# A Mamba and mixture-of-experts layer on one core: gelu's bias, the last sequence's logits and the start of the sixth expert group

## The chip, the core and the metric

The kernel runs on one core of a Trainium2 chip. The metric is the device time of one execution in microseconds; of several runs the median is given. The profile comes from one further execution, recorded by the hardware.

## What is computed

Sixteen sequences of 512 tokens with 256 features pass through two layers. All is in fp32.

```python
# layer 1: bidirectional state-space block (inner width 512, 16 states)
xf, res = split(x @ in_proj_w.T)
xf = silu(causal_conv(xf));  y = ssm(xf) * silu(res)
xb = silu(causal_conv_b(xf)); y = y + ssm_reversed(xb) * silu(res)
x = layernorm(x + y @ out_proj_w.T)
# layer 2: soft mixture of 16 experts, 64 slots each (1024 slots)
xn = layernorm(x) * norm_g + norm_b
se = (layernorm(slot_embeds) * slot_g + slot_b) * scale
logits   = einsum("bnd,esd->bnes", xn, se)
dispatch = softmax(logits, over tokens)
combine  = softmax(logits, over all slots)
slots = einsum("bnd,bnes->besd", xn, dispatch)
gate = gelu(slots @ Wg + bg);  up = slots @ Wu + bu
eout = (gate * up) @ Wd + bd
x = layernorm(x + combine @ eout)
```

The same logits feed two softmaxes: dispatch normalizes over the tokens, combine over the slots.

## The kernel before

**The scan.** `seq_layers` walks through the sequences 0 to 15. Each has four parts, `scan_part`: two directions for each half of the 512 channels. A part has eight pairs of states times two channel blocks, so a sequence has 64 scan steps. In a step ScalarE (ACT) makes decays and tanh factors (L453, L455), GpSimd (POOL) two products of 128x1024 elements (L436, L465), VectorE (DVE) the scans (L459, L461) and a product (L464), and TensorE (PE) turns the results and adds them up in PSUM (L380). A matmul with a tile of zeros (L376) opens each accumulator.

**Work beside the scan.** Everything else is written as generators, which `Side` objects hold in three queues: `prep` (the next scan part's inputs), `front` (`finish`: output projection, normalization, then `dispatch`) and `back` (`experts` and `combine`). After each scan step `beside_scan` lets them take a piece. `front` and `back` are paced: a queue's credit grows at each step by its remaining pieces over the remaining steps, which `begin(n)` sets. Instructions marked `late` stay in the order in which the program issues them; the scheduler places the others.

**Groups.** The experts of two sequences are done together: group g holds the sequences 2g and 2g+1. When the loop is at sequence b, `back` is given group (b-2)//2 at b = 3, 5, ..., 13 and, as a special case, the sixth group at b = 14: `experts(g, 0, 8)` (eight pairs of experts), then the combination of both sequences. `back.begin` gets 128 steps at odd b, 100 at b = 14, 64 at b = 15. In the last sequence (`hurry`) gaps between pieces aren't kept.

**One pair of experts.** Weights are loaded by SyncE's queue (SP), 512 KB each, into three buffers in the scan. `pg`: a matmul of the bias rows with a pattern of ones from the identity (L847), then the slots times Wg (L852). ACT makes the gelu of 128x512 (L869, L872). `pu`: the slots times Wu (L796). DVE adds bu and multiplies (L808). `peo`: times Wd (L823). DVE adds bd (L888) and the result goes to DRAM (L889). The slots `st` come from DRAM into a single buffer (L779).

**Logits.** `dispatch` computes them with the slots on the partitions, eight blocks `pl` of 128 slots x 512 tokens (L699), takes the maximum (DVE, L704), exp (ACT, L710), reciprocal and scale, turns the result (L716) and multiplies by the tokens (`pq`, L731); the slots go to DRAM as `sl`. `weights`, for the combination, computes the logits once more with the tokens on the partitions: for 128 tokens two halves `cl` of 512 slots (L906) from x2, which `finish` stored to DRAM and `load_x2` brings back. Then maxima (L914, L915), exp (L920), a turn `ctp` (L927), a copy `ct` (L936), and `combine` multiplies by the experts' outputs, `cpo` (L988), adds x1 (L997) and normalizes.

**The tail.** After the scan its PSUM and SBUF are given back: eight PSUM banks and eight weight buffers (`wide`) are then there. `front` still has `finish` and `dispatch` of sequence 15, `all_weights` of 14 and 15 (all turned weights kept) and the combination of 15; `back` has what is left of group 6, `experts` of group 7 and the combination of 14. Both are taken up in turn without pacing.

Of the kernel before, what the change touches and what calls it, by code (L numbers as in the profile page):

```python
# [9 lines left out]
F32 = mybir.dt.float32  # L10
# [7 lines left out]
P = 128  # L18
L = 512
# [36 lines left out]
def seq_layers(tc, ident, neghalf, a, out):  # L56
# [22 lines left out]
    with ExitStack() as ctx:  # L79
# [49 lines left out]
            return tc.keep_in_program_order(ins)  # L129


        zeros = const.tile([P, L], BF16, name="zeros")
        nc.vector.memset(zeros, 0.0)

        unit = const.tile([XW, 1], F32, name="unit")
# [234 lines left out]
        def add_up(depth):  # L370
            while len(pending) > depth:
                first, unit, last, c, hc, accs, w, u, name, done = pending.pop(0)
                if first:
                    accs[c] = ps_acc.tile([P, L], F32, tag="acc", name=name)

                    late(nc.tensor.matmul(accs[c], zeros[:, :P], zeros, start=True, stop=False))  # L376
                for j in range(2):
                    for lc in range(NL):
                        s = slice(lc * P, (lc + 1) * P)
                        ins = nc.tensor.matmul(  # L380
                            accs[c][:, s],
                            hc[:, j, s],
                            ident,
                            is_transpose=True,
                            start=False,
                            stop=(last and j == 1 and lc == NL - 1),
                        )
# [174 lines left out]
        def moe_setup():  # L562

            sg, sb = channels(a["slot_g"], "slot_g"), channels(a["slot_b"], "slot_b")
            scale = const.tile([P, 1], F32, name="scale")
            nc.sync.dma_start(scale, a["scale"].unsqueeze(0).to_broadcast([P, 1]))
            for t in (sg, sb):
                late(nc.vector.tensor_scalar(t, t, scale, None, ALU.mult))
            ses, src = [], a["slot_embeds"].rearrange("e s d -> (e s) d").rearrange("(h c p) d -> h p c d", p=P, c=4)
            for h in range(NSC // 4):  # L570
                se = p2.tile([P, 4 * DM], F32, tag="W", name=f"se_{h}", bufs=3)
                se = se.rearrange("p (c d) -> p c d", c=4)
                nc.sync.dma_start(se, src[h])
                ses.append(se)
            yield 0
            stats = [factors(row_moments(nc, p2, se, "m1", late), "m1") for se in ses]
            yield 0
            for se, (rs, sh) in zip(ses, stats):
                scaled(se, se, sh, rs)
            for k in range(NM):  # L580
                for h in range(NSC // 4):
                    yield 1
                    pt = bank(f"pse_{k}_{h}")
                    for j in range(4):
                        nc.tensor.transpose(pt[:, j * P : (j + 1) * P], ses[h][:, j, k * P : (k + 1) * P], ident)
# [6 lines left out]
            for key in ("bu",):  # L592
                rows = p2.tile([NE * NF, P], F32, tag="fr", name=f"{key}_rows")
                nc.sync.dma_start(rows, a[key].rearrange("e (c p) -> (e c) p", p=P))
# [6 lines left out]
                biases[key] = t  # L601

        def factors(mv, tag):

# [17 lines left out]
        def finish(b, y):  # L622
# [50 lines left out]
            for k in range(NM):  # L673
# [13 lines left out]
            yield from dispatch(b, xn, x2T)  # L687

        dispatched = {}
        expert_done = set()  # L690

        def dispatch(b, xn, x2T):

            for sc in range(NSC):
# [58 lines left out]
        def experts(g, lo, hi):  # L753
# [52 lines left out]
            def times(e, ht, pu):  # L806
                for fc in range(NF):
                    ins = nc.vector.scalar_tensor_tensor(  # L808
                        ht[:, fc, :],
                        pu[:, fc * P : (fc + 1) * P],  # L810
                        biases["bu"][:, e * NF + fc : e * NF + fc + 1],
                        ht[:, fc, :],
                        ALU.add,
                        ALU.mult,
                    )
                    if fc == 0:
                        late(ins)
# [15 lines left out]
            for ep in range(lo, hi):  # L833
# [5 lines left out]
                    yield WAIT  # L839
                yield 2  # L840
                pgs = []
                for j in range(2):
                    e = e0 + j
                    pg = bank(f"pg_{g}_{e}")

                    own = ident[: NE * NF, e * NF : (e + 1) * NF].unsqueeze(2).to_broadcast([NE * NF, NF, P])
                    nc.tensor.matmul(  # L847
                        pg.rearrange("p (f s) -> p f s", f=NF), biases["bg"], own, start=True, stop=False
                    )
                    for fc in range(NF):  # L850
                        for k in range(NM):
                            nc.tensor.matmul(  # L852
                                pg[:, fc * P : (fc + 1) * P],
                                got["Wg", e][:, k, fc * P : (fc + 1) * P],
                                st[:, k, :, j * SL : (j + 1) * SL],
                                start=False,
                                stop=(fc == NF - 1 and k == NM - 1),
                            )
                    pgs.append(pg)
                used[0] += 2  # L860
# [36 lines left out]
        def weights(b, lc, x2, keep):  # L897

            i = f"{b}_{lc}"
            yield 2  # L900
            t = x2.pop()
            cls = []
            for h in range(2):
                cl = bank(f"cl_{i}_{h}")
                for k in range(NM):
                    nc.tensor.matmul(  # L906
                        cl, t[:, k, :], seT[:, k, h * 512 : (h + 1) * 512], start=(k == 0), stop=(k == NM - 1)
                    )
                cls.append(cl)
            if lc + 1 < NL:  # L910
# [31 lines left out]
            return cts, sm[:, 2:3]  # L942

        def all_weights(b, kept):
            x2 = [load_x2(b, 0)]
            yield 0
            for lc in range(NL):
                kept[b, lc] = yield from weights(b, lc, x2, True)
# [72 lines left out]
        for b in range(nb):  # L1021
            bwd, nxt, accs = {}, {}, {}


            if 3 <= b < nb - 1 and b % 2 == 1 or b == nb - 2:
                g = (b - 2) // 2
                back.add(8 * PAIR, experts(g, 0, 8))
                back.add(COMBINE, combine(2 * g))
                back.add(COMBINE, combine(2 * g + 1))
            hurry = b + 1 == nb  # L1030
            front.begin(64)
            back.begin(128 if b % 2 == 1 and b + 1 < nb else 100 if b == nb - 2 else 64)

            def gate(c, b=b, accs=accs, bwd=bwd):
                y = bwd["res"]
# [85 lines left out]
```

## Time and profile before

| what | us |
|---|---|
| median of 3 runs | 5352.24 (5351.16 to 5356.49) |
| profiled execution | 5353.58 |
| its span, first to last instruction | 5351.8 |
| POOL busy | 4680.8 |
| DVE busy | 4551.7 |
| PE busy | 4331.0 |
| ACT busy | 4089.7 |
| last scan result added up (L1036) | 5100.7 |

The span is the time from the first to the last instruction; the execution's own time is 1.8 us longer. Busy time says how long an engine had instructions running; a matmul's end is modelled and neighbouring matmuls overlap, so starts are the safer measure on PE. `128x512` in a row is partitions by elements; `xN` counts instructions. One fp32 matmul of the program stands as two in the profile, a transpose as one. `<-` in a row of waits names what ended the wait.

### The profile page before, as it was taken

To read this page: it belongs to the slowest core of one execution; us is meant where nothing else is said; L and a number is where in the kernel's file an instruction comes from. 1 tells how busy PE (TensorE), PEld (TensorE's weight loads), DVE (VectorE), ACT (ScalarE), POOL (GpSimd) and SP (SyncE) were. 2 spreads that over 40 slices of the span, in tenths; PEclk is the share of its full clock that TensorE was granted. 3 is DMA by queue.
4 is the path that set the end of the run, shared out by engine and by line. 5 is a ranking of instruction groups with operands and counts; after the bars stand their busy time and mean duration, and the time that the engine had idled before them with its cause. 6 is when DMAs were issued, how large, how long until landed. Compare 5 with 4: busy or idle time off the path is not lost. (4 is left out here: it accounts for less than half of the span.)

```text
span 5351.8 us, 74548 instructions
## 1 busy us (share of the span) xinstructions
PE 4331.0 (81%) x24529; PEld 3407.3 (64%) x24529; DVE 4551.7 (85%) x6276; ACT 4089.7 (76%) x6518; POOL 4680.8 (87%) x2537
## 2 busy tenths in 40 slices
PE   5667776897778878798787988889787887888889
PEld 3556565766567766676666766676666766566667
DVE  7999999889898899889898898988999888887722
ACT  6778878887778878788787878888787887776633
POOL 6999999989999899998999999998999989987700
PEclk7788888998989989899899988999888998989999
DMA  5444444674446744566446754467444673456454
GB/s 144 136 130 150 125 146 135 211 231 147 146 150 223 224 131 146 184 219 198 132 144 206 229 161 157 143 211 231 149 146 149 222 227 127 140 180 217 146 162 140
DMA packets 616180, 908.86 MB, mean 170 GB/s; under 512 B 84687, under 2 KB 405839, under 8 KB 615793
## 3 DMA queue, kind: packets, MB, share of 16 engines
q1 hardware_dynamic: 533828, 859.88, 51.0%
q10 hardware_dynamic: 81964, 44.22, 3.1%
q8 instruction: 195, 3.19, 0.2%
q14 instruction: 193, 1.57, 0.1%
HBM read 840.86 MB, written 63.09 MB: 169 GB/s over the span
## 5 line engine op out<-in xcount | busy, mean ns | idle before, releaser
L465 POOL TENSOR_TENSOR hg<-hg,cs 128x1024 f32<-128x1024 f32 x1024 | 2421.6, 2369 | 143.2 <-DVE hg L464 108.6
L436 POOL TENSOR_TENSOR db<-du,bs 128x1024 f32<-128x1024 f32 (+1 forms) x1024 | 2092.1, 2047 | 225.7 <-issue 78.6
L464 DVE SCALAR_TENSOR_TENSOR hg<-th,h 128x512 f32<-128x512 f32 x1744 | 1158.5, 681 | 185.3 <-PE acc L380 112.1
L380 PE MATMUL acc<-ident,hg 128*128 128x128 f32 x8192 | 1157.9, 291 | 111.1 <-POOL hg L465 88.5
L380 PEld LDWEIGHTS acc<-ident,hg 128*128 128x128 f32 x8192 | 1029.6, 152 | 290.3 <-POOL hg L465 129.1
L461 DVE TENSOR_TENSOR_SCAN h<-h,db 128x512 f32<-128x512 f32 x872 | 1044.9, 1221 | 105.0 <-ACT h L453 95.4
L459 DVE TENSOR_TENSOR_SCAN h<-h,db 128x512 f32<-128x512 f32 x872 | 1045.7, 1221 | 47.7 <-ACT h L453 46.1
L455 ACT ACTIVATE th<-rr,Ah_f 128x512 f32<-128x512 f32 x1024 | 724.2, 714 | 206.0 <-DVE hg L464 200.5
L455 ACT ACTIVATE th<-rr,Ah_b 128x512 f32<-128x512 f32 x1024 | 721.3, 712 | 148.7 <-DVE hg L464 136.2
L453 ACT ACTIVATE h<-dt,A_f 128x512 f32<-128x512 f32 x872 | 591.5, 680 | 104.8 <-DVE hg L464 101.7
L453 ACT ACTIVATE h<-dt,A_b 128x512 f32<-128x512 f32 x872 | 592.3, 680 | 88.3 <-DVE hg L464 84.8
L414 PE MATMUL hd<-dg,duT 128*128 128x128 f32 x2432 | 371.1, 302 | 83.1 <-ACT duT L364 27.1
L414 PEld LDWEIGHTS hd<-dg,duT 128*128 128x128 f32 x2432 | 342.6, 217 | 94.4 <-ACT duT L364 28.9
L699 PE MATMUL pl<-x2T,seT 128*128 128x512 f32 x512 | 285.3, 685 | 72.0 <-DVE hg L464 32.4
L823 PE MATMUL peo<-Wd,ht 128*128 128x256 f32 x1024 | 262.5, 412 | 59.2 <-DVE rr L346 38.3
L852 PEld LDWEIGHTS pg<-st,Wg 128*128 128x128 f32 x2048 | 239.6, 192 | 99.6 <-issue 91.6
L796 PE MATMUL pu<-st,Wu 128*128 128x128 f32 x2048 | 258.2, 286 | 52.9 <-DMA Wu<-in_Wu_dram 24.2
L796 PEld LDWEIGHTS pu<-st,Wu 128*128 128x128 f32 x2048 | 248.4, 200 | 64.3 <-DVE h L461 24.6
L988 PE MATMUL cpo<-ceo,ct 128*128 128x256 f32 x1024 | 249.9, 400 | 34.0 <-DVE rr L346 33.5
L906 PE MATMUL cl<-seT,cx 128*128 128x512 f32 x512 | 245.7, 620 | 37.4 <-DVE res L277 10.3
L823 PEld LDWEIGHTS peo<-Wd,ht 128*128 128x128 f32 x1024 | 207.8, 208 | 105.5 <-DVE rr L346 40.8
L852 PE MATMUL pg<-st,Wg 128*128 128x128 f32 x2048 | 263.8, 282 | 3.0 <-DMA Wg<-in_Wg_dram 2.3
(154 smaller groups left out, 6742.1 us busy)
## 6 DMA issues: line engine op xcount, KB each, us to landing
cs<-bc SPq DMA_DIRECT2D x512, 512.0 KB, 3.7
bs<-bc SPq DMA_DIRECT2D x360, 512.0 KB, 4.8
Wg<-in_Wg_dram SPq DMA_DIRECT2D x128, 512.0 KB, 5.1
Wu<-in_Wu_dram SPq DMA_DIRECT2D x128, 512.0 KB, 5.7
Wd<-in_Wd_dram SPq DMA_DIRECT2D x128, 512.0 KB, 5.7
dg<-diag_dram SPq DMA_DIRECT2D x152, 256.0 KB, 4.1
bs<-bc SPq DMA_DIRECT2D x152, 256.0 KB, 3.6
x<-in_x_dram SPq DMA_DIRECT2D x32, 512.0 KB, 4.1
```

The costliest lines, as they stand in the source:

```text
L380: ins = nc.tensor.matmul(accs[c][:, s], hc[:, j, s], ident, is_transpose=True, start=False, stop=(last and j == 1 and lc == NL - 1),)
L414: ins = nc.tensor.matmul(h[:, s], v[c][3][:, s], dg[:, s], start=True, stop=True)
L436: nc.gpsimd.tensor_tensor(db[:, :k, :], du.unsqueeze(1).to_broadcast([P, k, L]), bs[:, :k, :], ALU.mult)
L453: nc.scalar.activation(hs[j][1], dt, AF.Exp, scale=w["A"][:, c, s])
L455: nc.scalar.activation(ths[j], rr, AF.Tanh, bias=LN_1E12 / 2, scale=w["Ah"][:, c, s])
L459: nc.vector.tensor_tensor_scan(h, dec, add, 0.0, ALU.mult, ALU.add)
L461: nc.vector.tensor_tensor_scan(h[:, ::-1], dec[:, ::-1], add[:, ::-1], 0.0, ALU.mult, ALU.add)
L464: nc.vector.scalar_tensor_tensor(hg[:, j, :], th, 1.0, h, ALU.add, ALU.mult)
L465: nc.gpsimd.tensor_tensor(hg, hg, cs, ALU.mult)
L796: nc.tensor.matmul(pu[:, fc * P : (fc + 1) * P], got["Wu", e][:, k, fc * P : (fc + 1) * P], st[:, k, :, j * SL : (j + 1) * SL], start=(k = ...
L823: nc.tensor.matmul(po[:, j * DM : (j + 1) * DM], ht[:, fc, :], got["Wd", e0 + j][:, fc, :], start=(fc == 0), stop=(fc == NF - 1),)
L852: nc.tensor.matmul(pg[:, fc * P : (fc + 1) * P], got["Wg", e][:, k, fc * P : (fc + 1) * P], st[:, k, :, j * SL : (j + 1) * SL], start=Fals ...
```

## The change

Five edits:

- **zeros** is 128x128 and is read four times over by a broadcast, instead of 128x512.
- **bg** is also turned once at the start, so that it stands in columns (one per expert and 128 hidden channels), like bu.
- **In the tail** the gelu gets its bias from those columns: no matmul for the bias, and four activations of 128x128 for each expert instead of one of 128x512. They are no longer marked `late`.
- **For sequence 15**, whose dispatch runs in the tail, each `pl` is copied by DVE to SBUF (into the buffers `xf` and `xb` of the scan). Its `weights` then turn the copied logits with 32 transposes instead of computing them with 16 matmuls. x2 of that sequence is neither stored nor loaded.
- **The sixth group** is begun at b = 15, with 64 steps, instead of at b = 14. The fifth then keeps sequence 14 to itself, with 64 steps left.

```diff
-        zeros = const.tile([P, L], BF16, name="zeros")
+        zeros = const.tile([P, P], BF16, name="zeros")
...
-                    late(nc.tensor.matmul(accs[c], zeros[:, :P], zeros, start=True, stop=False))
+                    late(nc.tensor.matmul(
+                            accs[c].rearrange("p (l s) -> p l s", l=NL),
+                            zeros,
+                            zeros.unsqueeze(1).to_broadcast([P, NL, P]),
+                            start=True,
+                            stop=False,
+                        ))
...
-            nc.scalar.dma_start(x2_dram[b].rearrange("k p l -> p k l"), x2T)
+            if not wide:
+                nc.scalar.dma_start(x2_dram[b].rearrange("k p l -> p k l"), x2T)
...
+                if wide:
+                    if sc == 0:
+                        logits[b] = [p1.tile([P, ND, L], F32, tag=t, name=f"logits_{b}_{t}") for t in ("xf", "xb")]
+                    nc.vector.tensor_copy(logits[b][sc // ND][:, sc % ND, :], pl)
...
+                by_tensor = not wide
...
+                    if by_tensor:
+                        own = ident[: NE * NF, e * NF : (e + 1) * NF].unsqueeze(2).to_broadcast([NE * NF, NF, P])
+                        nc.tensor.matmul(
+                            pg.rearrange("p (f s) -> p f s", f=NF), biases["bg"], own, start=True, stop=False
+                        )
...
-                                start=False,
-                                stop=(fc == NF - 1 and k == NM - 1),
+                                start=(not by_tensor and k == 0),
+                                stop=(k == NM - 1 and (not by_tensor or fc == NF - 1)),
...
-                    if j == 0:
+                    if not by_tensor:
+                        for fc in range(NF):
+                            i, s = e * NF + fc, slice(fc * P, (fc + 1) * P)
+                            nc.scalar.activation(
+                                ht[:, fc, :], pg[:, s], AF.Gelu, bias=biases["bg columns"][:, i : i + 1]
+                            )
+                    elif j == 0:
...
-                for k in range(NM):
+                for j in range(NSC // 2 if b in logits else 0):
+                    nc.tensor.transpose(
+                        cl[:, j * P : (j + 1) * P], logits[b][h][:, j, lc * P : (lc + 1) * P], ident
+                    )
+                for k in range(0 if b in logits else NM):
...
-            if 3 <= b < nb - 1 and b % 2 == 1 or b == nb - 2:
-                g = (b - 2) // 2
+            if b >= 3 and b % 2 == 1:
+                g = (b - 3) // 2
...
-            back.begin(128 if b % 2 == 1 and b + 1 < nb else 100 if b == nb - 2 else 64)
+            back.begin(128 if b % 2 == 1 and b + 1 < nb else 64)
```

More of the change, by code (lines that the diff above doesn't have):

```diff
@@ L591, in moe_setup @@
             nc.sync.dma_start(biases["bg"], a["bg"].rearrange("e (c p) -> (e c) p", p=P))
-            for key in ("bu",):
-                rows = p2.tile([NE * NF, P], F32, tag="fr", name=f"{key}_rows")
-                nc.sync.dma_start(rows, a[key].rearrange("e (c p) -> (e c) p", p=P))
+            for key in ("bu", "bg"):
+                if key == "bg":
+                    rows = biases["bg"]
+                else:
+                    rows = p2.tile([NE * NF, P], F32, tag="fr", name=f"{key}_rows")
+                    nc.sync.dma_start(rows, a[key].rearrange("e (c p) -> (e c) p", p=P))
                 yield 1
@@ L600, in moe_setup @@
                 nc.scalar.copy(t, pt[:, : NE * NF])
-                biases[key] = t
+                biases[f"{key} columns"] = t
         def factors(mv, tag):
@@ L685, in finish @@
                 )
-            nc.scalar.dma_start(x2_dram[b].rearrange("k p l -> p k l"), x2T)
+            if not wide:
+                nc.scalar.dma_start(x2_dram[b].rearrange("k p l -> p k l"), x2T)
             yield from dispatch(b, xn, x2T)
+        logits = {}
         dispatched = {}
@@ L810, in times @@
                         pu[:, fc * P : (fc + 1) * P],
-                        biases["bu"][:, e * NF + fc : e * NF + fc + 1],
+                        biases["bu columns"][:, e * NF + fc : e * NF + fc + 1],
                         ht[:, fc, :],
@@ L844, in experts @@
                     pg = bank(f"pg_{g}_{e}")
[L846 to L849, printed above, removed]
+                    if by_tensor:
[3 more added lines that the diff above has]
+                        )
                     for fc in range(NF):
@@ L900, in weights @@
             yield 2
-            t = x2.pop()
+            t = x2.pop() if x2 else None
             cls = []
@@ L909, in weights @@
                 cls.append(cl)
-            if lc + 1 < NL:
+            if t is not None and lc + 1 < NL:
                 x2.append(load_x2(b, lc + 1))
@@ L944, in all_weights @@
         def all_weights(b, kept):
-            x2 = [load_x2(b, 0)]
+            x2 = [] if b in logits else [load_x2(b, 0)]
             yield 0
```

## The prediction

> **What bounds the kernel now.** I read the page's busy shares first, then cut the span into stretches: POOL's multiply at L465 runs 64 times for each sequence, so every 64th of its starts in POOL's timeline is where a sequence begins. The busy table over those stretches (columns: length; PE, weight loads, DVE, ACT, POOL busy with instruction counts; granted clock, DMA share, GB/s) is the view that the whole working rests on.
>
> ```profile
> span 5351.8 us, 74548 instructions
> PE 4331.0 (81%) x24529; PEld 3407.3 (64%) x24529; DVE 4551.7 (85%) x6276; ACT 4089.7 (76%) x6518; POOL 4680.8 (87%) x2537
> ```
> ```profile
> 3442.50:3769.50 327.00, 283.25 (x1739) 230.28 (x1738) 284.18 (x398) 261.52 (x398) 295.33 (x157) 0.94 0.67 214
> 3769.50:4077.80 308.30, 244.64 (x1266) 185.18 (x1266) 282.21 (x384) 247.09 (x414) 295.01 (x157) 0.87 0.45 140
> 4077.80:4404.00 326.20, 282.93 (x1752) 229.55 (x1751) 283.87 (x398) 262.43 (x401) 295.32 (x157) 0.94 0.68 214
> 4404.00:4722.30 318.30, 241.24 (x1263) 179.67 (x1262) 281.39 (x385) 245.25 (x412) 296.58 (x162) 0.90 0.45 140
> 4722.30:5090.30 368.00, 312.24 (x1821) 250.51 (x1820) 281.89 (x410) 257.52 (x410) 281.69 (x145) 0.92 0.58 185
> 5090.30:5141.20 50.90, 46.89 (x214) 34.92 (x213) 14.82 (x42) 16.21 (x36) 6.97 (x12) 0.95 0.35 117
> 5141.20:5161.30 20.10, 13.80 (x45) 7.85 (x43) 2.89 (x8) 9.76 (x20) 0.34 (x2) 0.92 0.30 90
> 5161.30:5287.40 126.10, 126.10 (x732) 98.63 (x732) 31.03 (x91) 45.53 (x74) 0.00 (x0) 1.00 0.71 221
> 5287.40:5351.80 64.40, 58.12 (x277) 44.44 (x276) 18.76 (x54) 19.24 (x38) 9.71 (x32) 0.97 0.22 58
> ```
>
> Rows 1 to 5 are sequences 11 to 15. Sequences alternate: 327 us with a group's experts beside the scan, 308 us with its combinations. POOL, with about 295 us of work, sets those. Two rows break the pattern: sequence 14 takes 318 us, 15 takes 368. The last four rows are the tail, about 260 us: from 5161 to 5287 PE is busy all the time and POOL not at all. So there a PE instruction less is time less; in the scan it is not.
>
> The timeline shows one pair of experts of the tail (start, length, engine, line):
>
> ```profile
> 5265.48 3.60 PE L906 MATMUL cl<-seT,cx 128*128 128x512 f32 x8
> 5269.01 1.12 PE L847 MATMUL pg<-ident,bg_rows 64*128 64x512 f32 x2
> 5270.06 2.05 PE L852 MATMUL pg<-st,Wg 128*128 128x128 f32 x16
> 5272.04 1.12 PE L847 MATMUL pg<-ident,bg_rows 64*128 64x512 f32 x2
> 5273.10 2.05 PE L852 MATMUL pg<-st,Wg 128*128 128x128 f32 x16
> 5274.98 1.04 PE L927 MATMUL ctp<-ident,cm 128*128 128x128 f32 x8
> 5275.86 3.74 PE L796 MATMUL pu<-st,Wu 128*128 128x128 f32 x32
> 5279.43 3.60 PE L906 MATMUL cl<-seT,cx 128*128 128x512 f32 x8
> 5282.87 3.62 PE L823 MATMUL peo<-Wd,ht 128*128 128x256 f32 x16
> ```
>
> Lengths overlap, so I price by start to start: a bias product 5270.06 - 5269.01 = 1.05 us; the logits of a 128-token part, L906, 5282.87 - 5279.43 = 3.44; eight transposes, L927, 5275.86 - 5274.98 = 0.88, or 0.11 each; both `pu` 3.57; `peo` 3.45.
>
> **What the skill says.** *ScalarE: Activation LUTs*, section "What ACT_TABLE_LOAD costs": an activation takes 186 ns + 0.833 ns a column, 280 + 0.833 with a pointer bias, and neighbours overlap by 93 ns. The trace's gelu (L869), 597 ns for 512 columns without pointer, fits (612). The same section's 1283 ns table load is the trace's too. *TensorE: Matmul & The Clock Gate*, section "Back-to-back issue gap", has 216 ns for 512 columns; L906 here advances 3.44/8 = 430 ns a pass in fp32, so I use the trace. *DMA: Bandwidth & Descriptors*, "Anatomy of one DMA", puts a fixed cost near 2 us on a transfer, mostly its receipt; here the load of slots, `st`, lands 3.5 us after issue, and that is used.
>
> **The change, part by part.** The instruction order of the changed program, built and not run, agrees with that of before on PE until sequence 14, but for one transpose in sequence 0. I count from it.
>
> *Bias by ScalarE, PE's side.* Sixteen products of 1.05 us go. The first pair's two are worth nothing: PE runs them at 5140.56 while it waits for the softmax of the last sequence's dispatch, and its next real step waits for `st` (idle 0.70 us at 5161.27). Fourteen count: 14.7 us. What is late next: `st` has one buffer, its second load leaves at 5169.10 when `pu` of the first pair is done and lands about 3.5 us later, 5172.6 (longest seen 4.0); today the second pair's products start at 5173.53, without bias they would at 5172.48. That costs 0.1 to 0.6, take 0.4. In the later pairs `cl`, `pl`, `pq` or `ctp` stand between, with over 1 us of slack. Net -14.3.
>
> *ACT's side.* Four gelus of 128 columns with a pointer bias: 4 x (387 - 93) + 93 = 1.27 us, for 0.60. Over 16 experts +10.7 us on an engine busy 45.5 of 126 us. Cover: PE's 3.57 us of `pu`; the second expert's gelu ends 1.3 us after its `pg`. Without the cover it is 0.67 x 8 pairs = 5.4 us; taken as 0. Queued behind them on ACT are copies of `pd` and the exps of `cl`; PE asks for those 4 us later. The order holds as many table loads as before. A gain is excluded: ACT only gets more.
>
> *Logits kept.* Eight copies of 128x512 from PSUM on DVE. No row shows one; L704's reduction of the same block takes 0.69 us, so 5.5 us in all, 5.5 if exposed, 0 if hidden. Each stands between the maximum and the reciprocal, which waits for the exp (0.69 + 0.19 us) anyway: 0. One store of `x2` leaves ACT's queue and four loads of 128 KB SP's; nothing waits for them now: 0. The logits lie in `xf` and `xb`, whose last readers (L393) ended at 5039.
>
> *Turning instead of multiplying.* Four times 3.44 - 0.88 = 2.56 us. The first lies in the saturated stretch: -2.56. The other three follow the last `peo`, where something else is near:
>
> ```profile
> 5301.27 3.62 PE L823 MATMUL peo<-Wd,ht 128*128 128x256 f32 x16
> 5305.64 0.36 SPq L889 DMA_DIRECT2D e_dram<-eo  x1
> 5307.77 1.25 SPq L963 DMA_DIRECT2D ceo<-e_dram  x2
> 5313.33 1.89 PE L988 MATMUL cpo<-ceo,ct 128*128 128x256 f32 x8
> ```
>
> The experts' output goes through DRAM, and PE fills 5304.7 to 5313.3 with `cl`, `cpo` and `ctp`. In the new order the fill before that `cpo` is 8.3 us (others moved up), but `ctp` waits for its softmax: two maxima 1.4 us, two exps 1.7. Stepping through it I find PE at that `cpo` 9.2 us after the last `peo`, and 1 us of waiting later. So 7.7 - 2.0 = -5.7. Together -8.3.
>
> *ACT's order at the tail's start.* Three normalizations of sequence 13 now stand ahead of the first exp of the dispatch instead of one: two of 0.52 us on a chain with no cover until 5161: +1.1.
>
> Tail: -14.3 - 8.3 + 1.1 = -21.5.
>
> *The sixth group begun later.* All its instructions move, SP's loads of weights, slots and `bd`, its stores of `e_dram`, POOL's and ACT's part of the combinations in front of it. In the new order sequence 14 holds what sequence 12 holds, quarter by quarter (`cl` 8, 8, 8, 8; it was 8, 4, 12, 4). Then 13 and 14 should take what 11 and 12 take, 327.0 + 308.3 = 635.3, against 326.2 + 318.3 = 644.5: -9.2. In sequence 15 the first pair's product starts at the 20th of the scan's steps and the last `peo` at the 57th, for 16th and 56th; its PE work is the same, since the first `pg` runs at 4731 already, but in 37 steps for 40. PE is busy 312 of 368 us there, the rest are waits that any order deals anew. I take +1.6, within -10 to +12. Sum -7.6.
>
> *Zeros by broadcast.* 64 products of 379 ns, of the same size. L847 reads a broadcast operand too, and its two passes' weight loads lie 0.43 us apart, as L906's: 0. Were each doubled, 24 us of PE, mostly beside POOL. The added transpose and copy in sequence 0: 0.2 us of ACT, beside the scan: 0.
>
> **Sum.** -21.5 - 7.6 = -29.1. The profiled execution took 5353.6 us (span 5351.8, 1.8 around it), so 5324.5; the median of the runs is 1.3 lower, 5352.2. I say 5324.
>
> **Rivals.** (1) Forecast, 5324. (2) *A new wait eats half the tail.* Exposed gelus 5.4, exposed copies 5.5: 5324 + 11 = 5335. For it: in-order ACT; against: 80 us of ACT idle in 126. (3) *The last sequence is squeezed.* It ends 12 us later, as an unlucky wait of 11.7 us (the longest in it now, PE for ACT's `et`) comes once more: 5336. (4) *Slower.* In sequence 15 weights have three buffers. PE waited there for `Wd` 7.5 us in three times; if all eight pairs expose the whole 5.7 us from issue to landing, +45.6: 5370. It decides from 29.1/8 = 3.6 us a pair; against it, those eight pairs meet it now too and pay 4.4 at most once. (5) *Better.* Sequence 15 loses its wait of 11.7 us: 5312. (6) *No turn*, if the changed order doesn't hold in the scan and 14 keeps its 318: 5333.
>
> **Chances.** Forecast 0.55, (2) 0.12, (3) 0.12, (4) 0.04, (5) 0.10, (6) 0.07. The range 5307 to 5341 takes (5) with 5 us of margin and (3) with 5. A measurement of this kernel tells about 0.2%, 11 us, from no change. Faster by more, below 5341.5: 0.90; within: 0.06; slower: 0.04, case (4).
>
> **What would show it.** Right: no L847-like products in the tail, pairs of experts about 2.1 us apart less (19.5 to 17.4) with PE still fully busy; sequence 14 near 308; four turns of 0.9 us. Wrong: PE idle before `peo` for DVE's product of gate and up (gelu late), before `pg` for `st` by more than 1 us in several pairs; sequence 15 over 380.

## The result, and the profile after

| | before, us | changed, us | ratio and 95% interval |
|---|---|---|---|
| first comparison (6 and 6 runs) | 5353.41 | 5330.25 (5322.25 to 5338.24) | 0.9959, 0.9946 to 0.9971 |
| second, another chip (9 and 5 runs) | 5351.72 | 5328.03 (5326.76 to 5331.41) | 0.9957, 0.9944 to 0.9969 |

The ratio is estimated from the single runs, so it need not be the quotient of the two medians. By the ratios the change is 22.0 us faster (15.5 to 28.9), and 23.0 (16.6 to 30.0) in the second comparison; the medians differ by 23.2 and 23.7. The forecast was 29.1 faster, 5324, within 5307 to 5341: the time lies in the range, and the forecast gain at the upper edge of the intervals. The profiled execution of the changed kernel took 5322.25 us. It is the lowest of its six runs, so its total flatters the change, and below I compare pieces of it and not its sum.

The lines of the page and the table of stretches that answer to those of before (same columns; rows 1 and 2 are sequences 14 and 15, the others the tail, cut at 53 us after the scan's last POOL product, at the first `pg` of the experts, and at the end of the stretch in which PE is full):

```profile
span 5320.5 us, 74550 instructions
PE 4310.4 (81%) x24498; PEld 3411.1 (64%) x24498; DVE 4560.6 (86%) x6284; ACT 4104.9 (77%) x6573; POOL 4681.6 (88%) x2537
```
```profile
4401.00:4709.70 308.70, 244.63 (x1270) 185.01 (x1269) 282.58 (x384) 247.47 (x414) 295.13 (x157) 0.87 0.46 140
4709.70:5077.70 368.00, 309.25 (x1817) 247.78 (x1814) 282.65 (x412) 263.61 (x413) 283.36 (x150) 0.93 0.59 188
5077.70:5130.70 53.00, 47.46 (x215) 34.19 (x213) 15.82 (x44) 18.47 (x41) 7.33 (x13) 0.97 0.32 107
5130.70:5150.60 19.90, 11.73 (x36) 7.61 (x37) 4.36 (x10) 8.14 (x16) 0.00 (x0) 0.83 0.25 79
5150.60:5268.80 118.20, 116.34 (x735) 99.93 (x736) 33.50 (x95) 54.71 (x121) 0.00 (x0) 0.99 0.77 238
5268.80:5320.50 51.70, 43.63 (x247) 37.69 (x245) 18.35 (x53) 17.43 (x38) 9.71 (x32) 0.97 0.23 59
```

Sequence 14 now takes 308.70 us (318.30 before) and has the PE, DVE and ACT work that sequence 12 had. Sequence 15 takes 368.00 again. In the full stretch PE is busy 116.34 of 118.20 us, and ACT 54.71 (it was 45.53 of 126): room enough. The last pair of experts of the changed tail (start, length, engine, line):

```profile
5265.80 3.74 PE L869 MATMUL pg<-st,Wg 128*128 128x128 f32 x32
5269.38 0.60 PE L929 MATMUL cl<-ident,logits_xf 128*128 128x128 f32 x4
5269.81 0.60 PE L929 MATMUL cl<-ident,logits_xb 128*128 128x128 f32 x4
5270.25 3.74 PE L811 MATMUL pu<-st,Wu 128*128 128x128 f32 x32
```

The bias products are gone: the 32 products of `pg` take 5269.38 - 5265.80 = 3.58 us in one run. Before, the pair took 5274.98 - 5269.01 = 5.97. So an edit that was priced at 2 x 1.05 us brings 2.39 a pair: by the starts in the trace the first product behind each bias product takes 0.21 us to its follower instead of 0.11, and so does the last product in front of the second bias product. The turn of 128 tokens' logits takes 5270.25 - 5269.38 = 0.87 us.

Where the tail's gain went shows when the tail is cut in three, from the last product of the scan (`res`, L1036 before, L1062 after): *start*, up to the ninth product of the first pair's `pu`; *full*, from there to the last `peo`; *end*. All from the starts in the traces:

| us | start | full | end | tail |
|---|---|---|---|---|
| before | 65.1 | 138.7 | 47.3 | 251.1 |
| changed | 69.5 | 121.4 | 42.3 | 233.2 |
| changed, second profile | 70.8 | 121.9 | 41.7 | 234.4 |
| difference (first profile) | +4.4 | -17.3 | -4.9 | -17.9 |

Full and end came as forecast. The start, which should have lost 1.1, lost 4.4. PE's lines there, before:

```profile
5149.02 0.66 PE L716 MATMUL pd<-ident,et 128*128 128x128 f32 x4 [2.55 <-ACT et L712]
5150.35 5.30 PE L731 MATMUL pq<-dis,xn 128*128 128x256 f32 x16 [0.67 <-ACT dis L721]
5155.49 3.60 PE L699 MATMUL pl<-x2T,seT 128*128 128x512 f32 x8
...
5161.27 0.68 PE L852 MATMUL pg<-st,Wg 128*128 128x128 f32 x4 [0.70 <-DMA st<-s_dram]
```

and after (the bracket is PE's idle time in front and what ended it):

```profile
5137.13 1.12 PE L731 MATMUL pd<-ident,et 128*128 128x128 f32 x4 [3.14 <-ACT et L727]
5138.92 6.08 PE L746 MATMUL pq<-dis,xn 128*128 128x256 f32 x16 [0.68 <-ACT dis L736]
...
5145.27 1.88 PE L710 MATMUL pl<-x2T,seT 128*128 128x512 f32 x4
5150.60 5.42 PE L869 MATMUL pg<-st,Wg 128*128 128x128 f32 x32 [3.45 <-DMA st<-s_dram]
```

Three things are to be seen. The second turn `pd` waits 3.14 us for the softmax instead of 2.55. Between `pq` and `pg` PE has one block of logits left (`pl` x4) where it had two (x8), since the scheduler did one of them earlier; it idles 3.45 us for `st` instead of 0.70. And the same work takes longer: the turn 1.12 us for 0.66, `pq` 6.08 for 5.30, the 32 `pg` 5.42 where later pairs take 3.74. The granted clock says why. The table of stretches has it as the third number from the right; over the first `pg` it was 1.00 before (first line) and is 0.73 after (second).

```profile
5161.20:5165.80 4.60, 4.53 (x40) 4.56 (x41) 0.00 (x0) 2.72 (x4) 0.00 (x0) 1.00 0.12 32
```
```profile
5150.60:5156.80 6.20, 6.20 (x41) 6.20 (x42) 0.00 (x0) 2.83 (x8) 0.00 (x0) 0.73 0.23 21
```

Why the softmax is later, DVE and ACT tell. The maximum and the exp of the second block before:

```profile
5146.50 0.69 DVE L704 TENSOR_REDUCE nm<-pl 128x1 f32<-128x512 f32 x1 [3.38 <-PE pl L699]
5147.23 0.69 ACT L710 ACTIVATE et<-pl,nm 128x512 f32<-128x512 f32 x1 [1.17 <-DVE nm L704]
```

and after, DVE first, then ACT:

```profile
5134.02 0.69 DVE L715 TENSOR_REDUCE nm<-pl 128x1 f32<-128x512 f32 x1 [3.22 <-PE pl L710]
5134.63 0.68 DVE L723 COPY logits_xf<-pl 128x512 f32<-128x512 f32 x1
```
```profile
5128.36 1.58 ACT L625 ACTIVATE cx<-cx,c_sh,c_rs 128x256 f32<-128x256 f32 x3 [2.22 <-POOL c_sh L620]
...
5135.35 0.69 ACT L725 ACTIVATE et<-pl,nm 128x512 f32<-128x512 f32 x1 [2.25 <-DVE logits_xf L723]
```

The exp does not start when the maximum is there (the copy starts at 5134.63) but when the copy of the same PSUM block is done: it follows the maximum's start by 1.33 us (5135.35 - 5134.02), before by 0.73 (5147.23 - 5146.50). And the first exp stands behind three normalizations of sequence 13.

### The profile page after: what moved, and what is told of

The parts are those of the page before. It is cut to its first block, busy times and chain, and to the rows that moved or that the text cites. A ratio compares the mean times of both kernels' runs of the same rounds, so it can differ in the third digit from the quotient of the medians.

```text
span 5320.5 us, 74550 instructions
## 1 busy us (share of the span) xinstructions
PE 4310.4 (81%) x24498; PEld 3411.1 (64%) x24498; DVE 4560.6 (86%) x6284; ACT 4104.9 (77%) x6573; POOL 4681.6 (88%) x2537
## 5 line engine op out<-in xcount | busy, mean ns | idle before, releaser
L471 POOL TENSOR_TENSOR hg<-hg,cs 128x1024 f32<-128x1024 f32 x1024 | 2416.9, 2364 | 125.0 <-DVE hg L470 108.0
L420 PE MATMUL hd<-dg,duT 128*128 128x128 f32 x2432 | 375.7, 305 | 73.2 <-ACT duT L364 27.1
L1015 PEld LDWEIGHTS cpo<-ceo,ct 128*128 128x128 f32 x1024 | 207.2, 207 | 87.2 <-DVE rr L346 42.7
```

The source lines that it names most:

```text
L420: ins = nc.tensor.matmul(h[:, s], v[c][3][:, s], dg[:, s], start=True, stop=True)
L471: nc.gpsimd.tensor_tensor(hg, hg, cs, ALU.mult)
L1015: nc.tensor.matmul(po[:, :DM], cts[sc // 4][:, sc % 4 * P : (sc % 4 + 1) * P], eos[sc // 4][:, sc % 4, :], start=(sc == 0), stop=(sc == NS ...
```

## The experiments

"Tail" is from the last scan product to the end, as in the table above. The lengths of stretches come from one profiled execution of each kernel and have no interval.

**The parts alone.** All four kernels ran on one chip beside the kernel before, whose median there was 5352.6 us.

*The group alone*: the kernel before with the group's new place and nothing else.

```diff
-            if 3 <= b < nb - 1 and b % 2 == 1 or b == nb - 2:
-                g = (b - 2) // 2
+            if b >= 3 and b % 2 == 1:
+                g = (b - 3) // 2
...
-            back.begin(128 if b % 2 == 1 and b + 1 < nb else 100 if b == nb - 2 else 64)
+            back.begin(128 if b % 2 == 1 and b + 1 < nb else 64)
```

> The kernel before with the sixth group begun at b = 15 and nothing else. Theory A (sequence 14 becomes an ordinary one, 15 is as long as it was): sequence 14 at 308 to 309 us for 318, 15 at 368, tail 261: about -9 us in the profile and in the median. Rival R (the profile of the changed kernel caught a lucky last sequence; the experts in 37 steps make it longer in most executions): 14 at 308, but 15 at 373 to 380, so the median moves by -4 to +3 and the runs spread over more than 10 us.

*The tail alone*: the same two edits undone in the changed kernel.

> The changed kernel with the sixth group begun as before, at b = 14. Theory A: the tail alone gives its 18 to 19 us (261.5 to 243 from the last scan product to the end), scan as before, so -18 in profile and median with a spread as narrow as before's (9 us). Rival R says the same of the tail, and the narrow spread, since the wide one comes from the group. If the median is nearer -12, the tail's profile gain isn't got in every execution and the shortfall of the change lies in the tail.

*The bias alone*, in the tail (the changed kernel with the group undone, no copies, logits multiplied again):

```diff
-            if not wide:
+            if True:
                 nc.scalar.dma_start(x2_dram[b].rearrange("k p l -> p k l"), x2T)
...
-                if wide:
+                if False:
                     if sc == 0:
```

> The kernel before with only gelu's bias by ScalarE in the tail (bias columns made at the start, small zeros tile). By the record's step: 14 products of 1.05 us less, 14.3. By the profile of the changed kernel: pairs 2 to 8 give 14.4, the start of the tail takes back what the idle PE's clock costs (1.5 us) since PE then waits longer before the first pair: -12 to -13 us. If the loss at the tail's start is due to the bias being gone, it is here; if it is due to the order of ACT's normalizations or the copies, it is in logits_only.

*The logits alone* (the changed kernel with the group undone, bias by PE again):

```diff
-                by_tensor = not wide
+                by_tensor = True
```

> The kernel before with only the last sequence's logits kept and turned. By the record: -8.3 for the four turns, +1.1 if ACT's order at the tail's start belongs to it: -7 us. First turn 2.56, the other three 5 to 6 between them, with PE waiting for the softmax before one of the ctp. The eight copies on DVE cost nothing.

| | median, us | against before: by the ratio, by the medians | ratio, 95% | start | full | end | tail |
|---|---|---|---|---|---|---|---|
| group alone | 5347.03 | -5.9, -5.6 | 0.9983 to 0.9996 | 65.0 | 138.8 | 47.3 | 251.1 |
| tail alone | 5334.67 | -18.2, -17.9 | 0.9954 to 0.9979 | 69.4 | 121.8 | 42.3 | 233.4 |
| bias alone | 5338.63 | -13.4, -14.0 | 0.9964 to 0.9985 | 68.1 | 122.7 | 47.6 | 238.4 |
| logits alone | 5349.23 | -5.3, -3.4 | 0.9982 to 0.9998 | 69.3 | 136.3 | 41.7 | 247.3 |

The group and the tail add up: 5.9 + 18.2 = 24.1 by the ratios and 23.5 by the medians, for 22.0 and 23.2 in the first comparison of the whole change. For the group neither expectation came as stated: in its one profile sequence 14 took 310.5 us and sequence 15 372.2, and the median moved by a value between the two. Within the tail, the bias brings 16.0 in the full stretch, the logits 2.4 there and 5.6 in the end; each by itself loses 3.0 and 4.2 at the start, and both together only 4.4. So the start's loss isn't a price of the copies alone. The bias alone has no copy, and its first exp stands behind one normalization, as before; its second turn comes as before (48.4 us after `res`, 48.3 before), and yet:

```profile
5146.90 1.12 PE L731 MATMUL pd<-ident,et 128*128 128x128 f32 x4 [2.55 <-ACT et L727]
...
5160.34 5.50 PE L869 MATMUL pg<-st,Wg 128*128 128x128 f32 x32 [3.37 <-DMA st<-s_dram]
```

The turn takes 1.12 us for 0.66, and the `pg`, again behind a wait of over 3 us for `st`, 5.50. Turn, `pq` and `pg` together are about 3.0 us slower: here the loss is clock.

**The bias products as filler.** The first pair's products by PE again, since their two microseconds stood in front of the first turn.

```diff
-                by_tensor = not wide
+                by_tensor = not wide or ep == lo
```

> The changed kernel, but the first pair of the tail has its bias by matmul as before (four passes of PE work back, into PE's wait for the dispatch). Theory C (the clock: without that work PE is idle longer, the granted clock falls to half once more and the first pg run at half speed, 6.15 us from the first pg to the ninth pu for 4.54): half-clock time back from 10.2 to 3.4 to 6.8 us, 4.5 to 5 us there, tail 1.5 us shorter although it does more. Rival (the clock falls because the wait itself grew, by the copies and ACT's order): still 6.1 us, tail the same or up to 0.5 longer.

The products do stand there (5138.35 to 5140.3), and PE's wait before the first turn falls from 2.58 to 0.67 us. Nothing else moves: start 69.4, tail 233.2, `pg` 5.44 us (one execution, 5331.66). The idea that they kept PE's clock up falls.

**ACT's pieces without PE's saving.** Bias by PE everywhere, and the gelu of the tail still in four pieces, with a pointer to zero.

```diff
-                by_tensor = not wide
+                by_tensor = True
...
-                    if not by_tensor:
+                    if wide:
                         for fc in range(NF):
...
-                                ht[:, fc, :], pg[:, s], AF.Gelu, bias=biases["bg columns"][:, i : i + 1]
+                                ht[:, fc, :], pg[:, s], AF.Gelu, bias=zero[:, 0:1]
```

> The changed kernel with the tail's bias back on PE, while ACT still makes each gelu in four pieces of 128 columns with a pointer bias (a column of zeros): the cost of the pieces by itself. On record: +10.7 us of ACT work, nothing on the path. Then the stretch from the ninth pu of the first pair to the last peo is as in the kernel with the logits alone, 136.3 us, and the tail 247.3. Rival (pieces exposed): up to 5.4 us more.

Full 136.3 and tail 247.4, as with the logits alone (136.3, 247.3): four pieces cost nothing on the path (one execution, 5347.41).

**The copy behind the exp.**

```diff
-                if wide:
-                    if sc == 0:
-                        logits[b] = ...
-                    nc.vector.tensor_copy(logits[b][sc // ND][:, sc % ND, :], pl)
                 sm = p3.tile([P, 1], F32, tag="sm", name=f"sm_{i}")
                 nc.scalar.activation(et, pl, AF.Exp, bias=nm, accum_out=sm)
                 nc.vector.reciprocal(sm, sm)
                 nc.scalar.activation(et, et, AF.Identity, scale=sm)
+                if wide:
+                    ...
```

> The changed kernel with the copy of the logits placed behind the exp and its scaling in the program, so that DVE does maximum, reciprocal, copy. In the changed kernel the exp begins as the copy ends, 1.33 us after the maximum's start, where it was 0.73 before. Theory A (the exp waits for the copy, 0.6 us each time; the record took it as free): from the last scan product to the first pq 51.0 us or less for 51.64, the exp again 0.73 us after the maximum; the tail 0.6 to 1.2 us shorter. Rival B (exp and copy can't read the same PSUM block together, or the exp is late for another reason): no change, 51.6.

The exp follows the maximum at 0.73 us again (5142.90 - 5142.17), and the wait of the second turn is 2.55 us again. But the half clock came earlier in this execution and lasted longer, so that the start took 70.7 us. The gain shows elsewhere, in the full stretch, 120.2 for 121.9 in the second profile of the changed kernel. PE's waits for a turn in the 126 us from just behind the start of the first `pg`, copy ahead of the exp (second profile of the changed kernel; columns: us in all, times, longest):

```profile
PE pd L731 <- ACT et L727: 1.8, 2, 0.9
```

and copy behind it:

```profile
PE pd L731 <- ACT et L723: 0.3, 1, 0.3
```

So two of the copies ahead were exposed for 0.9 us each in pairs that have no bias products left to stand in front of the turn: the third and fourth intervals from one pair's `pg` to the next take 17.34 + 13.88 us in all profiles that have the bias on ACT and the copies ahead of the exp (seven profiles of six kernels, to 0.01 us), and 16.21 + 13.28, 1.73 less, in the three without: this one, its sibling below, and the bias alone, which has no copies. With the logits alone, where the bias products still stand in those pairs, there is no such wait. One execution: 5328.79.

**Without sequence 13's normalizations** (left out: four activations that finish its output, which stays unnormalized there):

```diff
-                scaled(x1[:, lo:hi, :], x1[:, lo:hi, :], sh, rs)
+                if not (wide and kept is None):
+                    scaled(x1[:, lo:hi, :], x1[:, lo:hi, :], sh, rs)
```

> The changed kernel without ACT's four last normalizations of sequence 13 in the tail; its output is then not normalized. What the order of ACT at the tail's start costs: on record 1.1 us, as two more of them stand ahead of the first exp. Theory A: first pq 1.1 to 1.6 us earlier than in the changed kernel, 50.0 to 50.6 for 51.64 (three are gone, but the exp then waits for the maximum). Rival: POOL's factors don't matter to the exp, 51.6. Like the other three this also shows how long the last sequence is with the sixth group begun in it: 368 to 372 if theory A holds, against 363.5 to 368.1 with the group begun earlier.

The first exp starts 41.39 us after `res`, for 42.56: 1.17 earlier, and what it waits for now is the copy. The first `pq` comes 1.6 us earlier (50.0 for 51.6), the first `pg` 2.5 (60.8 for 63.3). The half clock took 1.2 of that back over `pg` (7.4 us to the ninth `pu` instead of 6.2), and the start is 68.2. The full stretch was 122.7 here, so the tail is 232.5, only 0.7 below the changed kernel's (one execution, 5336.05, with a sequence 15 of 372.0).

**The third block of logits back in its place, the pace of the sixth group, and the changed kernel again**, beside one another on another chip (before: 5351.72):

```diff
-                    nc.tensor.matmul(
+                    ins = nc.tensor.matmul(
                         pl, seT[:, k, sc * P : (sc + 1) * P], x2T[:, k, :], start=(k == 0), stop=(k == NM - 1)
                     )
+                    if wide and k == 0:
+                        late(ins)
```

> The changed kernel with the first matmul of each of the tail's logits blocks (pl, L710) kept in the program's order, so that the third block, which the changed program does ahead of the first turn pd, comes back to between the first pq and the experts' first pg, where it stood before. Theory D (TensorE has nothing to do between pq and pg, waits 3.5 us for the slots, and its clock falls again): its wait before the first pg goes from 3.45 to about 1 us, the half clock after it goes, the first pair's gate takes 4.5 us to the first pu instead of 6.2, and the tail is 1.5 us shorter than the changed kernel's 233.2: about 231.7. Rival (the clock falls for another reason, or the slots come as late and the half clock stays): 6.2 and 233.2 again. In the median 0 to 2 us below the changed kernel.

The same with the copies behind the exp:

> As pl_in_order, and the copy of the logits issued after the exp, so that the exp follows the maximum at 0.73 us again. If the exp's wait for the copy lies on the chain at the tail's start and nothing eats the gain, the first pg comes 0.6 us earlier than in pl_in_order and the tail is about 231; if the half clock eats it, as it did in copy_after_exp, the tail is that of pl_in_order. Median about 2 us below the changed kernel where both hold, 0 where neither does.

```diff
-            back.begin(128 if b % 2 == 1 and b + 1 < nb else 64)
+            back.begin(128 if b % 2 == 1 and b + 1 < nb else 56 if b + 1 == nb else 64)
```

> The changed kernel with the sixth group's experts in the last sequence paced over 56 of its scan steps instead of 64. Squeeze theory (sequence 15 is 3.2 us longer in the changed kernel because the eight pairs of experts stand in fewer scan steps): sequence 15 longer by another 2 to 6 us, 371 to 375, and at most 1 us off the tail; median 1 to 5 us slower than the changed kernel. Rival (sequence 15's length is dealt anew from order to order and isn't the pace's): sequence 15 within 366 to 370.

> The changed kernel itself once more, beside the others on one chip, since its profiled execution was the lowest of its runs. If the sum of its parts holds (tail 17.9 us shorter, sequences 13 to 15 together 5 us shorter), its median is 21 to 25 us below the kernel before; if the profiled execution was the typical one, 29 to 31 below.

| | median, us (range) | ratio, 95% | start | full | tail | sequence 15 |
|---|---|---|---|---|---|---|
| changed again | 5328.03 (5326.76 to 5331.41) | 0.9944 to 0.9969 | 70.8 | 121.9 | 234.4 | 366.4 |
| `pl` in order | 5331.54 (5328.95 to 5333.15) | 0.9948 to 0.9976 | 73.2 | 121.3 | 236.4 | 366.4 |
| and copy after exp | 5326.59 (5324.38 to 5329.80) | 0.9941 to 0.9966 | 71.2 | 120.0 | 233.3 | 369.0 |
| pace 56 | 5324.30 (5321.39 to 5326.89) | 0.9936 to 0.9961 | 69.5 | 121.1 | 232.7 | 365.6 |

My theory of the order came true in its first half and failed in its result. With `pl` in order, PE no longer waits for `st`:

```profile
5137.09 1.12 PE L733 MATMUL pd<-ident,et 128*128 128x128 f32 x4 [4.29 <-ACT et L729]
...
5157.63 0.66 PE L733 MATMUL pd<-ident,et 128*128 128x128 f32 x4 [3.14 <-ACT et L729]
...
5159.27 5.10 PE L871 MATMUL pg<-st,Wg 128*128 128x128 f32 x32
```

But the wait is now in front of the turns: 4.29 us for the first, where the second `pl` had stood, and 3.14 for the third, which in the kernel before came behind two blocks `pl` and not one. (The order of before isn't fully restored: there the fourth block stood beside the third.) The tail grew by 2.0 us over the changed kernel's second profile. With the copies behind the exp the last gap is 2.55 us and that `pg` runs at full clock, 3.77 us for 32 products. But the half clock came after this gap too: it fell on the block of logits between, whose four passes take 3.58 us where they took 1.88:

```profile
5154.21 0.67 PE L733 MATMUL pd<-ident,et 128*128 128x128 f32 x4 [2.55 <-ACT et L725]
5154.71 3.58 PE L710 MATMUL pl<-x2T,seT 128*128 128x512 f32 x4
5158.09 3.77 PE L871 MATMUL pg<-st,Wg 128*128 128x128 f32 x32
```

So its start is 71.2 us: the clock was half for 13.7 us from the 43rd microsecond on and for 3.4 here. Its median is 1.4 us below that of the changed kernel, which five runs of each don't tell apart. Against `pl` in order alone, where only the place of the copies differs, it is 5.0 us lower, with ranges that overlap by 0.9.

The edit of the pace didn't make the experts denser. Counted by POOL's 64 products of sequence 15 (L471), the first pair's `pg` starts behind the 5th instead of the 6th, that of the other seven pairs behind the same ones as in the changed kernel (the last behind the 42nd), and the last `peo` behind the 44th in both. So this run doesn't test the squeeze theory. That kernel has the lowest median of all, 3.7 us below the changed kernel's beside it, with ranges that just touch; the profile shows 0.8 of it in sequence 15 and 1.7 in the tail, and 0.07% is less than what this measurement was said to tell.

## Why the prediction was right, and where it wasn't

The time fell in the range with the mechanism that was forecast. The time alone wouldn't show it: 5330.25 lies nearer to rivals (6), 5333, and (2), 5335, than to 5324. The stretches decide. Step by step, by the table of before and after:

- *Bias by ScalarE, PE's side, -14.3.* Measured with the bias alone, -16.0 in the full stretch. The term was too small: a bias product was priced at the 1.05 us to its follower, and costs 1.20 with the slow steps behind it and in front (2.39 a pair). The 0.4 us for the second `st` is there in some profiles (0.4 in the second of the changed kernel).
- *ACT's side, 0.* Right: the pieces without the saving cost nothing. They are also cheaper than the 1.27 us estimated from the Trainium skill (*ScalarE: Activation LUTs*, "What ACT_TABLE_LOAD costs"): four take 1.14 here.

```profile
5269.58 1.14 ACT L888 ACTIVATE ht<-pg,bg_cols 128x128 f32<-128x128 f32 x4 [0.54 <-PE pg L869]
```

- *Logits kept, "Each stands between the maximum and the reciprocal, which waits for the exp (0.69 + 0.19 us) anyway: 0".* This step failed. The copy and the exp read the same PSUM block, and the exp, queued behind the copy, waits for it: 0.6 us on the chain at the start, and 1.7 us in the full stretch. The Trainium skill has what I should have read: *PSUM — Partial Sum Buffer*, "PSUM bank collisions raise a hardware error", says that no two engines may touch the same 32-partition quarter of a bank at once, two reads included, and that the compiler's scheduler therefore adds a dependency between such instructions of ACT and DVE. The trace agrees as far as it goes: ACT's wait ends with L723, and with the copy behind the exp that wait is gone. That the shared block, and not only the order on DVE, is what makes the exp wait was not tried with two different blocks. Rival (2) named this cost, with 5.5 us exposed; a little under half of that was measured.
- *Turning instead of multiplying, -8.3.* -2.4 in the full stretch and -4.9 to -5.6 in the end: right. `ctp` waits for its softmax there for 1.19 us, as stepped through, and the first `cpo` behind the last `peo` 0.39 for its data.
- *ACT's order at the tail's start, +1.1.* Right for what it names: the first exp was 1.10 us later against `res` than before, and without the normalizations it was 0.07 earlier. But it was taken for all that happens at the start, and the start lost 4.4. On the chain, in the first profile: the first turn +0.9 by the normalizations, the second +0.6 by the copy; then the turn +0.45, `pq` +0.8 and `pg` +1.6 by the clock. This is the term that carried most of the error of the tail, -17.9 for -21.5: 2.85 of clock and 0.6 of copy that were not in the sum.
- *The sixth group begun later, -9.2 and +1.6.* Sequences 13 and 14 took 636.8 us in the mean of nine profiles with the new place at pace 64 (634.8 to 637.8), 644.8 in four with the old one: -8.0. Sequence 15 took 368.6 (366.4 to 372.2) for 366.1 (363.5 to 368.1): +2.5. Together -5.5, and -5.9 by the times of the group alone, for -7.6. The gain in 13 and 14 and its cause are right, off by about a microsecond. The loss in 15 is not clear of the scatter, as the ranges overlap, and what causes it is not shown. Sequence 14 did not always take what sequence 12 takes: 308.3 to 308.7 us in three of the nine profiles, 310.5 in six, and 308.7 and 310.5 in the two of one kernel. Why is open; other even sequences show the same step in some executions. And the wait of 11.7 us that rivals (3) and (5) put into sequence 15 was read into the wrong sequence: PE's wait, in brackets below, ends at 4721.78, and POOL's first product of sequence 15 starts at 4722.26.

```profile
4721.78 1.11 PE L716 MATMUL pd<-ident,et 128*128 128x128 f32 x4 [11.68 <-ACT et L712]
```

  It stands there in all four profiles with the old place of the group, and in none of the ten with the new one, where PE's longest wait in the two sequences is 6.4 us (8.0 at pace 56). What it alone was worth to sequence 14 was not separated.
- *Zeros by broadcast, 0.* Right: the 64 products have a median of 379 ns before and after, and 216 ns to the product behind. The reading that led there was wrong: the two weight loads of a bias product (L847) lie 0.11 us apart in 126 of 128 cases, not 0.43, and its two passes start 0.53 us apart where those of L906 start 0.43 apart.

That the full stretch came as forecast (-17.3 for -16.9) was in part luck: the bias brought 1.7 us more than its term and the exposed copies took 1.7 back.

Sum of the measured parts: -17.9 - 5.5 = -23.4, for -22.0 and -23.0 by the ratios and -23.2 and -23.7 by the medians. Rivals (4), weights exposed, and (6), no turn, fall. Of (3), the squeeze by 12 us, there is at most the 2.5 us in the mean; whether those come from the denser experts stays open. Rival (5) falls too: the long wait is gone, but it lay in sequence 14, whose gain the forecast already counts, and sequence 15 is no shorter.

**When the clock falls.** In the first profile it was half for 10.2 us of the 30 us around the start, in the second profile of the same kernel for 17.1, before for 3.4, by the trace's record of the granted clock; each stretch is 3.4 us long or a multiple. The Trainium skill (*TensorE: Matmul & The Clock Gate*, "What's actually happening") has a window of about 3.4 us that runs free of the program, at whose end the clock follows how busy PE was. The traces agree, and the busy times of these windows say more than any single gap. The changed kernel, first profile (one line for each window; PE's busy time is the number behind the comma, the granted clock the third from the right):

```profile
5130.08:5133.50 3.42, 1.89 (x8) 1.07 (x8) 0.16 (x1) 2.33 (x5) 0.00 (x0) 1.00 0.13 48
5133.50:5136.91 3.41, 0.48 (x2) 0.00 (x0) 2.04 (x5) 1.33 (x3) 0.00 (x0) 1.00 0.41 120
5136.91:5140.32 3.41, 2.52 (x7) 1.90 (x8) 0.76 (x2) 1.97 (x5) 0.00 (x0) 0.50 0.40 140
5140.32:5143.73 3.41, 3.41 (x9) 2.70 (x8) 0.00 (x0) 0.18 (x1) 0.00 (x0) 0.50 0.00 0
5143.73:5147.15 3.42, 3.42 (x14) 1.91 (x12) 0.00 (x0) 1.02 (x2) 0.00 (x0) 1.00 0.04 15
5147.15:5150.56 3.41, 0.01 (x1) 0.00 (x0) 1.45 (x3) 1.79 (x4) 0.00 (x0) 1.00 0.44 139
5150.56:5153.98 3.42, 3.38 (x16) 3.41 (x17) 0.00 (x0) 0.99 (x1) 0.00 (x0) 0.50 0.00 0
```

and the second profile, in which the windows lie 0.7 us earlier against the last scan product; the window with the gap before the first turn holds 1.19 us of PE work where it held 1.89, and half clock follows it:

```profile
5135.95:5139.37 3.42, 1.19 (x6) 0.88 (x7) 0.16 (x1) 2.73 (x7) 0.00 (x0) 1.00 0.00 0
5139.37:5142.78 3.41, 2.24 (x3) 0.34 (x1) 1.13 (x2) 0.29 (x1) 0.00 (x0) 0.50 0.45 156
```

In the tails of all fourteen profiles the busy time of one window tells the clock of the next without an exception. Of 914 windows at full clock, the 41 in which PE was busy for 41% or less were followed by half clock, the 873 with 48% or more by full clock. Of 48 at half clock, the 21 with 83% or less were followed by half clock again, the 27 with 88% or more by full. So where the windows happen to lie has a part in what a gap costs, and filling the gap before the first turn changed nothing, since the window of the second turn stayed as empty as it was. In the scan half clock followed 1999 of 2005 windows that were busy for less than 42%, but also 449 of 14492 fuller ones, so busy time is not all that counts there. This is a regularity in the traces, and not an experiment on the windows.

**What stays open.** Why sequence 14 takes two lengths, what sequence 15 loses, and an order that would fill the gaps at the start without lengthening another.

## What to carry to other kernels

A copy that "only" hangs on a buffer another engine is about to read is not free: look up which of the two was issued first, and put the one on the chain first. Price what is taken out of a saturated stretch by the time from the end of what stands in front to the start of what stands behind, not by its own row. And where an edit thins out the work of PE in a stretch full of waits, the next work may run at half clock: add up PE's busy time over the 3.4 us windows of the trace, keep a microsecond or two each way for where they fall, and compare parts of the trace rather than the total of one execution.

## What was not expected of the hardware

- PE at half clock comes and goes in stretches of 3.4 us, and the same program had 10.2 and 17.1 us of it at one place in two executions; the tail differed by 1.2 us. In the tails the clock fell after every window in which PE was busy for 41% or less, and after none with 48% or more.
- Filling 1.9 us of a 2.6 us gap with products didn't change the later clock, while each gap of 3.3 to 3.5 us in front of the first `pg` was followed by half clock; a gap of that length left 0 to 27% of a window busy.
- A matmul of 64x512 among 128x128 ones costs 0.15 us beyond its own 1.05.
- ACT takes four pieces of 128 columns with a pointer bias in 1.14 us and eight in 2.17, so 0.26 us for each further one; one piece of 512 without pointer took 0.60.
